# First blocks of one, two, three and four chunks on two queues, and the weight loads of the first stage moved behind them

## The chip, the cores and the metric

The kernel runs on one core of a Trainium2 chip. The metric is device time in microseconds (us), the median of several runs; lower is better. The engines are TensorE (PE: matmuls, with PEld for its weight loads), VectorE (DVE), ScalarE (ACT), GpSimd (POOL) and SyncE (SP). DMAs are issued from SP, from ACT and from POOL; in the profile SPq and ACTq are the issuing queues.

## The reference, cut to what matters

`x` is 2708 x 256 and `adj` a sparse 2708 x 2708 matrix, both float32. Four graph layers follow one another, each with a residual and a layernorm. Only the first and the start of the second matter here:

```python
# layer 0
x = _layernorm(x + adj @ (x * W0), axis=-1)
# layer 1 (graph attention, 4 heads of 64)
h = (x @ W).reshape(n, heads, head_dim)
src = einsum('nhd,d->nh', h, a[:head_dim, 0])
dst = einsum('nhd,d->nh', h, a[head_dim:, 0])
e = leaky_relu(src[:, :, None] + dst.T[None, :, :])     # masked by adj > 0, softmax, times h
x = _layernorm(x + _layernorm(out) * gamma + beta)
```

Layer 2 is three attention heads and two GRU cells, with weights `gat_W`, `gat_a` and biases `bih`, `bhh`; layer 3 is a mean over neighbours with two linear maps, `neigh_W` and `lin_W`.

## The kernel before, in words

Rows are cut into 22 tiles of 128 (the last has 20). The transposed adjacency comes in strips: strip t is 128 partitions x 22 chunks x 128 columns (1.44 MB), and layer 0 of row tile t is 22 matmuls of its chunks with the 22 chunks of x (`x0e`, kept in the tile `turn` with a column of ones for the degrees). A float32 matmul is two passes in the profile, so a strip is 44 passes.

Names and lines (those of the kernel before):

- L396 `w1_a` (ACT queue): W of layer 1, loaded first of all; L443 `w0_b`: W0 in all partitions; L498 `a1_b`: the attention vector; L215/L513 `wk`, `ak`: three heads' `gat_W` and `gat_a`; L233 `braw` in `gru_columns`: four bias vectors turned into columns, 3 KB each in pieces of 4 bytes. All these are issued from ACT before its first computation.
- L502/L509 fold `a1_b` into `w1_a` and L515/L516 make `uw` from `wk` and `ak`, on DVE; L234 to L239 make the bias columns `b_edge`, `b_node`.
- L524, L529 and L531, the prologue: for each block of four chunks SP loads the chunks of x and then the same chunks of strips 0, 1 and 2 (`ahead = 3`); L533 are their matmuls, L451 the mask (`adj > 0`) on DVE. Six blocks: five of four chunks, one of two.
- `layer0_own`: L458 takes the diagonal, L465 `below` makes six ACT passes over a strip that sum what is negative, 0.62 to 0.75 us each.
- L539: strip 3 whole, then L215 `nw` and `lw`, the weights of layer 3, from SP. L548: POOL writes `lwn_d` from `lw`.
- L202 `load_strip`: strips 4 to 21, in the two buffers that strips 0 and 1 leave; L211 their matmuls.
- `layer0_rest`: the layernorm (L170 to L175, its power `bn_rs` on POOL, L481) and then `layer1_projection`: PE transposes the tile (L187), ACT copies it to `xt` (L189), PE multiplies by `w1_a` (L419 `pm`), ACT makes `rise`, `h`, `fall` (L422 to L425), PE transposes `fall` (L434 `pf`).

Each engine runs its instructions in one order, which the scheduler fixes when the program is built; on ACT the first copy to `xt` stands behind the `below` passes of strips 0 to 4 and behind two of strip 5. The DMAs of SP and ACT take eight completion semaphores in turn, so each of them first waits until the DMA eight places before it, on whichever of the two queues, has landed. Instructions that the scheduler has moved apart from their place in the text are in the profile under the same lines.

Of the kernel before, what the change touches and what calls it, by code (L numbers as in the profile page):

```python
# [27 lines left out]
def kernel(  # L28
# [39 lines left out]

    sizes = [NT // -(-NT // GT) + (i < NT % -(-NT // GT)) for i in range(-(-NT // GT))]
    spans = [(sum(sizes[:i]), sum(sizes[: i + 1])) for i in range(len(sizes))]  # L70
    blocks = [(c, min(c + CB, NT)) for c in range(0, NT, CB)]


    NH, MH = N // 2, NT // 2
# [13 lines left out]
    def sz(i):  # L88
        return min(P, N - i * P)
# [4 lines left out]
    def bcast(row, n):  # L94
        return bass.AP(tensor=row.tensor, offset=row.offset, ap=[[0, P], [1, n]])
# [113 lines left out]
    def strip_matmul(acc, s, n, rhs):  # L209
        for c in range(NT):  # L210
            nc.tensor.matmul(acc, s[:, c, :n], rhs(c), start=(c == 0), stop=(c == NT - 1))  # L211

    def weights(pool, name, w, queue=nc.sync):
        wt = pool.tile([P, w.shape[0] // P, w.shape[1]], F32, name=name)
        queue.dma_start(wt, w.rearrange("(c p) j -> p c j", p=P))  # L215
        return wt
# [9 lines left out]
        nc.vector.tensor_tensor(y[:n], y[:n], pz[:n, :F], ALU.add)  # L226
        nc.scalar.dma_start(y3_d[t], y[:n])

    def gru_columns(pool, b, bih, bhh):

        raw = pool.tile([P, 2, 3 * FC], F32, tag="braw", name="braw", bufs=2)
        for i, src in enumerate((bih, bhh)):
            nc.scalar.dma_start(raw[:, i], src.rearrange("(c p) -> p c", p=P))  # L233
        nc.vector.tensor_tensor(raw[:, 0, : 2 * FC], raw[:, 0, : 2 * FC], raw[:, 1, : 2 * FC], ALU.add)  # L234
        nc.vector.tensor_scalar(
            b[:, 0:2].rearrange("p a c -> p (a c)"), raw[:, 0, : 2 * FC], 0.5, None, ALU.mult
        )
        nc.vector.tensor_scalar(b[:, 2], raw[:, 1, 2 * FC :], 0.5, None, ALU.mult)
        nc.vector.tensor_copy(b[:, 3], raw[:, 0, 2 * FC :])  # L239
# [153 lines left out]
    if True:  # L393

        w1_a = keep.tile([P, FC, F + 2 * H], F32, name="w1_a")
        nc.scalar.dma_start(w1_a[:, :, H : H + F], w1.rearrange("(c p) j -> p c j", p=P))  # L396

        hs = [keep.tile([P, H, HD + 1], F32, name=f"h{t}") for t in range(NT)]
        nc.gpsimd.memset(hs[NT - 1], 0.0)
# [7 lines left out]
        if True:  # L407
# [32 lines left out]
                    load_fall(falls[g // 2], g, nc.gpsimd)  # L440

            w0_b = keep.tile([P, F], F32, name="w0_b")
            nc.scalar.dma_start(w0_b, bcast(w0, F))  # L443
            quarter = keep.tile([P, CT], F32, name="quarter")
            nc.vector.tensor_reduce(quarter, ident.rearrange("p (j i) -> p i j", i=CT), AX.X, ALU.add)

            with pool("l0", 2) as l0:

                def layer0_mask(t, s, lo=0, hi=NT):
                    n = sz(t)  # L450
                    nc.vector.tensor_scalar(  # L451
                        mask[:, lo:hi, t * P : t * P + n], s[:, lo:hi, :n], 0.0, None, ALU.is_gt, saturate=False
                    )

                def layer0_own(t, s):
                    n = sz(t)
                    dtmp = st.rearrange("p t i k -> p (t i k)")
                    nc.vector.scalar_tensor_tensor(  # L458
                        dtmp[:n, :n], s[:n, t, :n], 1.0, ident[:n, :n], ALU.mult, ALU.mult,
                        accum_out=diag[:n, t : t + 1],  # L460
                    )
                    for i in range(BELOW):
                        lo, hi = i * NT // BELOW, (i + 1) * NT // BELOW
                        below = l0.tile([P, -(-NT // BELOW) * P], BF16, tag="below", name="below", bufs=1)
                        nc.scalar.activation(  # L465
                            below[:, : (hi - lo) * P], s[:, lo:hi].rearrange("p c n -> p (c n)"), AF.Relu, scale=-1.0,
                            accum_out=negative[:, BELOW * t + i : BELOW * t + i + 1],
                        )
# [25 lines left out]

                ahead = 3
                with pool("prep", side="right") as prep:
                    a1_b = prep.tile([P, 2 * HD], F32, name="a1_b")
                    nc.scalar.dma_start(a1_b, bcast(a1, 2 * HD))  # L498
                    for f in range(FC):
                        for s in range(2):  # L500
                            tmp = prep.tile([P, H, HD], F32, tag="t1", name="t1")
# [5 lines left out]
                            )  # L507
                            at = s * (H + F)
                            nc.vector.tensor_reduce(w1_a[:, f, at : at + H], tmp, AX.X, ALU.add)  # L509
                    for k in range(K):  # L510
                        wk = weights(prep, f"wk{k}", gat_w[k], nc.scalar)
                        ak = prep.tile([P, F], F32, name=f"ak{k}")
                        nc.scalar.dma_start(ak, bcast(gat_a[k], F))  # L513
                        tmp = prep.tile([P, FC, F], F32, tag="t2", name="t2")
                        nc.vector.tensor_tensor(tmp, wk, ak[:, None, :].to_broadcast([P, FC, F]), ALU.mult)  # L515
                        nc.vector.tensor_reduce(uw[:, :, k], tmp, AX.X, ALU.add)  # L516
                    gru_columns(prep, b_edge, e_bih, e_bhh)
                    gru_columns(prep, b_node, n_bih, n_bhh)
                    strips = [l0.tile([P, NT, P], F32, tag="strip", name="strip", bufs=2) for _ in range(2)]
                    strips += [prep.tile([P, NT, P], F32, name=f"strip{t}") for t in range(2, ahead + 1)]  # L520
                    accs = [ps_acc.tile([P, 512], F32, tag="acc", name="acc") for _ in range(ahead)]
                    for c0, c1 in blocks:
                        whole = min(c1, N // P)
                        nc.sync.dma_start(  # L524
                            turn[:, c0 * FE : whole * FE].rearrange("p (c f) -> p c f", f=FE)[:, :, :F],
                            x[c0 * P : whole * P, :].rearrange("(c p) f -> p c f", p=P),
                        )
                        for c in range(whole, c1):
                            nc.sync.dma_start(x0[c][: sz(c)], x[c * P : c * P + sz(c), :])  # L529
                        for t in range(ahead):  # L530
                            nc.sync.dma_start(strips[t][:, c0:c1], adj_t[t, :, c0:c1])  # L531
                            for c in range(c0, c1):
                                nc.tensor.matmul(  # L533
                                    accs[t][:, :FE], strips[t][:, c], x0e[c], start=(c == 0), stop=(c == NT - 1)
                                )
                            layer0_mask(t, strips[t], c0, c1)
                    for t in range(ahead):
                        layer0_own(t, strips[t])
                    nc.sync.dma_start(strips[ahead], adj_t[ahead])  # L539
                    for t in range(ahead):  # L540
                        layer0_scale(t, accs[t])
                    acc = ps_acc.tile([P, 512], F32, tag="acc", name="acc")
                    strip_matmul(acc[:, :FE], strips[ahead], P, lambda c: x0e[c])
                    for t in range(ahead):
                        finish(layer0_rest(l0, t))
                    nw = weights(prep, "nw", neigh_w)
                    lw = weights(prep, "lw", lin_w)
                    nc.gpsimd.dma_start(lwn_d[:, :, :F], lw[:, :FC])  # L548
# [1082 lines left out]
```

## Time and profile before

| what | value |
|---|---|
| median of 3 runs | 1880.27 us (1879.21 to 1880.66) |
| the profiled execution | 1881.39 us, of which the span is 1879.3 us |
| PE busy | 1840.5 us, 98% of the span |
| DVE, ACT, POOL busy | 1279.0, 689.0, 259.9 us |
| granted TensorE clock | 0.998 of full |
| DMA | 235.92 MB, mean 126 GB/s |
| PE busy in the first 15 us | 7.68 us |
| PE busy from 15 to 30 us, from 30 to 50 us | 13.94 of 15 us, 20.00 of 20 us |
| DMA in the first 30 us | 0.83 to 1.01 of the engines' time, 254 and 318 GB/s in the two halves |

Busy time is the union of an engine's instructions; matmuls overlap in their pipeline, so a matmul of 379 ns takes some 217 ns of PE's time in a row. An idle time of an engine is put down to what came last of what it waited for.

### The profile page before, as it was taken

What the parts mean: (1) busy time and instruction counts of PE and PEld (TensorE: products, weight loads), DVE (VectorE), ACT (ScalarE), POOL (GpSimd) and SP (SyncE); (2) the same over time, 40 slices, a digit from 0 to 9 for tenths busy, and PEclk for the clock granted to TensorE, in tenths of its full rate; (3) what the DMA queues carried; (4) which work ended last, traced back from release to release, by engine and by line L of the source; (5) the groups of instructions that cost most, each with busy time, mean ns of one, the idle gap of its engine ahead of it and who ended that gap; (6) DMA issues with size and microseconds to landing.
All of it is one profiled execution on the core that took longest, in us unless ns stands there. A gap on an engine that the chain in (4) does not pass through costs nothing.

```text
span 1879.3 us, 23102 instructions
## 1 busy us (share of the span) xinstructions
PE 1840.5 (98%) x7561; PEld 1035.5 (55%) x7565; DVE 1279.0 (68%) x2280; ACT 689.0 (37%) x1419; POOL 259.9 (14%) x419
## 2 busy tenths in 40 slices
PE   8999999999999999999999999999999999999997
PEld 7788842233345886887444444444445555554555
DVE  5343479999897655654658888776887758744664
ACT  4444410033144203111555665555564555311011
POOL 1211220001012411000011001210200202111111
PEclk9999999999999999999999999999999999999999
DMA  9344410100002657764557665454554445534764
GB/s 298 130 146 146 159 42 1 30 1 12 12 7 74 144 143 188 176 144 113 164 148 207 179 168 147 134 155 115 163 144 114 128 103 134 155 101 109 198 167 123
DMA packets 434204, 235.92 MB, mean 126 GB/s; under 512 B 184182, under 2 KB 421388, under 8 KB 431644
## 3 DMA queue, kind: packets, MB, share of 16 engines
q1 hardware_dynamic: 417438, 207.41, 40.5%
q0 software_dynamic: 7760, 21.20, 3.5%
q10 hardware_dynamic: 8878, 5.76, 1.0%
q8 instruction: 62, 1.02, 0.2%
q14 instruction: 66, 0.54, 0.1%
HBM read 221.61 MB, written 12.65 MB: 125 GB/s over the span
## 4 chain that ended last, share of the span: by engine, by line
PE 83%; DMA 5%; DVE 4%; issue 3%; ACT 2%; POOL 1%; SPq 1%; ACTq 0%; DVEq 0%; POOLq 0%
PE m L317 38%; PE acc L763 11%; PE bank L1128 7%; PE acc L211 7%; PE den L772 6%; PE gate L1003 4%; PE bank L1104 3%; DMA strip<-in_adj_t_dram 2%; PE bank L1179 1%; ACT below L465 1%; DMA p<-in_adj_t_dram 1%; SPq L264 1%; PE pm L419 1%; POOL bn_rs L175 1%; PE pq L929 1%
## 5 line engine op out<-in xcount | busy, mean ns | idle before, releaser
L781 DVE SCALAR_TENSOR_TENSOR p<-fall_b,rise,mask 128x1024 f32<-128x1024 f32 (+1 forms) x264 | 294.0, 1157 | 32.5 <-PE den L772 16.7
L1258 ACT ACTIVATE p<-st,e_neg 128x1024 f32<-128x1024 f32 (+1 forms) x198 | 197.1, 1040 | 193.7 <-PE m L317 186.3
L317 PE MATMUL m<-s,xq 128*128 128x512 f32 (+3 forms) x660 | 230.1, 467 | 0.0
L763 PE MATMUL acc<-p,h 128*64 128x512 f32 (+2 forms) x1056 | 214.5, 548 | 0.2 <-ACT sum L794 0.2
L317 PE MATMUL m<-p,xq 128*128 128x512 f32 (+1 forms) x396 | 182.8, 543 | 0.1
L211 PE MATMUL acc<-turn,strip 128*128 128x257 f32 x792 | 181.5, 379 | 0.0
L1261 ACT ACTIVATE p<-p 128x1024 f32<-128x1024 f32 (+1 forms) x198 | 178.9, 943 | 0.2
L1262 DVE TENSOR_TENSOR p<-p,blk 128x1024 f32<-128x1024 f32 (+1 forms) x132 | 143.6, 1107 | 39.7 <-ACT p L1261 24.3
L317 PE MATMUL m<-p,x 128*128 128x512 f32 (+1 forms) x396 | 167.8, 542 | 0.3 <-DVE supt L334 0.3
L304 DVE TENSOR_TENSOR s<-p 128x512 f32<-128x512 f32 (+3 forms) x132 | 81.1, 615 | 124.3 <-PE m L317 101.0
L317 PEld LDWEIGHTS m<-s,xq 128*128 128x128 f32 x660 | 124.3, 190 | 74.8 <-issue 57.6
L211 PEld LDWEIGHTS acc<-turn,strip 128*128 128x128 f32 x792 | 147.2, 190 | 20.3
L763 PEld LDWEIGHTS acc<-p,h 128*64 128x64 f32 x1056 | 69.8, 136 | 138.2 <-issue 128.6
L317 PE MATMUL m<-s,x 128*128 128x512 f32 (+3 forms) x330 | 127.3, 467 | 0.0
L772 PE MATMUL den<-p,h 128*32 128x512 f32 (+2 forms) x1056 | 117.7, 548 | 0.0
L317 PEld LDWEIGHTS m<-p,xq 128*128 128x128 f32 x396 | 74.6, 190 | 76.0 <-issue 61.4
L317 PEld LDWEIGHTS m<-p,x 128*128 128x128 f32 x396 | 74.4, 190 | 73.6 <-issue 61.2
L465 ACT ACTIVATE below<-strip 128x384 bf16<-128x384 f32 x132 | 78.5, 594 | 72.9 <-DMA strip<-in_adj_t_dram 69.5
L1262 DVE TENSOR_TENSOR p<-p,turn 128x1024 f32<-128x1024 f32 (+1 forms) x66 | 72.2, 1108 | 17.9 <-PE m L317 11.6
L305 DVE TENSOR_TENSOR p<-p 128x512 f32<-128x512 f32 (+3 forms) x132 | 82.4, 625 | 1.9
L307 DVE TENSOR_TENSOR s<-p,s 128x512 f32<-128x512 f32 (+3 forms) x132 | 81.5, 617 | 2.0
L317 PEld LDWEIGHTS m<-s,x 128*128 128x128 f32 x330 | 61.8, 190 | 38.1 <-issue 34.3
(276 smaller groups left out, 2541.1 us busy)
## 6 DMA issues: line engine op xcount, KB each, us to landing
strip<-in_adj_t_dram SPq DMA_DIRECT2D x19, 1408.0 KB, 6.0
blk<-in_adj_t_dram SPq DMA_DIRECT2D x88, 256.0 KB, 3.4
blk<-in_adj_t_dram SPq DMA_DIRECT2D x88, 192.0 KB, 4.0
pa<-in_adj_t_dram SPq DMA_DIRECT2D x110, 128.0 KB, 2.7
turn<-in_adj_t_dram SPq DMA_DIRECT2D x44, 256.0 KB, 3.3
blk<-in_adj_t_dram SPq DMA_DIRECT2D x88, 128.0 KB, 2.5
p<-in_adj_t_dram SPq DMA_DIRECT2D x88, 128.0 KB, 2.6
turn<-in_adj_t_dram SPq DMA_DIRECT2D x44, 192.0 KB, 3.1
```

What stands on the lines that cost most here:

```text
L211: nc.tensor.matmul(acc, s[:, c, :n], rhs(c), start=(c == 0), stop=(c == NT - 1))
L305: nc.vector.tensor_tensor(a21, a21, a11, ALU.subtract)
L307: nc.vector.tensor_tensor(s4, a12, s2, ALU.subtract)
L317: nc.tensor.matmul(dst[:, :w], lt, rt, start=start and not (one_bank and i), stop=stop and not (one_bank and i in (1, 2, 5)))
L465: nc.scalar.activation(below[:, : (hi - lo) * P], s[:, lo:hi].rearrange("p c n -> p (c n)"), AF.Relu, scale=-1.0, accum_out=negative[:, BE ...
L763: nc.tensor.matmul(acc[s][i * HD : (i + 1) * HD, :ws], hs[c][:, 2 * q + i, :HD], ps[i][:, p0 : p0 + ws], **flags,)
L772: nc.tensor.matmul(den[j : j + CT, :ws], hs[c][:, 2 * q + i, HD + 1 - CT :], ps[i][:, p0 : p0 + ws], **flags,)
L781: nc.vector.scalar_tensor_tensor(p[:, :w], falls[g // 2][:, 2 * q + i, :w], rise[:, c, 2 * q + i : 2 * q + i + 1], mask[:, c, at : at + w] ...
L1128: nc.tensor.matmul(g[:, :w], lt, rt, start=(q == 0), stop=(q == len(terms) - 1))
L1258: nc.scalar.activation(p[:, :, :w], st_k[:, :, :w], AF.Relu, scale=-1.0, bias=e_neg[:, at, k : k + 1])
L1261: nc.scalar.activation(p[:, :, :w], p[:, :, :w], AF.Exp, scale=-1.0)
L1262: nc.vector.tensor_tensor(p[:, :, :w], p[:, :, :w], blk[:, i, :, :w], ALU.mult)
```

## The change

The blocks become 1, 2, 3, 4, 4, 4, 4 chunks. The x chunks of the first two blocks are issued from ACT, all the rest from SP. The block loop is moved ahead of the weight preparation, and `w0_b`, then strip 3, then `w1_a`, `a1_b`, `wk`, `ak` and the biases are issued from SP behind the last block (`tc.issue_after` only fixes that order in the queue); `gru_columns` is cut in two, the loads (`gru_load`) and the arithmetic. The DVE arithmetic on the weights moves behind strip 3's mask. `nw`, `lw` and the strips from 4 on follow in SP's queue as before. In the new order of ACT, the first copy to `xt` stands behind the passes of strips 0 to 4 and four of strip 5; PE, POOL and the later parts of all engines keep their order but for one chunk of strip 4, which PE takes later.

```diff
--- before.py
+++ after.py
@@ -68,7 +68,8 @@
 
     sizes = [NT // -(-NT // GT) + (i < NT % -(-NT // GT)) for i in range(-(-NT // GT))]
     spans = [(sum(sizes[:i]), sum(sizes[: i + 1])) for i in range(len(sizes))]
-    blocks = [(c, min(c + CB, NT)) for c in range(0, NT, CB)]
+    cuts = [0, 1, 3, 6, *range(10, NT, CB), NT]
+    blocks = list(zip(cuts, cuts[1:]))
 
 
     NH, MH = N // 2, NT // 2
@@ -226,11 +227,15 @@
         nc.vector.tensor_tensor(y[:n], y[:n], pz[:n, :F], ALU.add)
         nc.scalar.dma_start(y3_d[t], y[:n])
 
-    def gru_columns(pool, b, bih, bhh):
+    def gru_load(pool, bih, bhh):
 
         raw = pool.tile([P, 2, 3 * FC], F32, tag="braw", name="braw", bufs=2)
         for i, src in enumerate((bih, bhh)):
-            nc.scalar.dma_start(raw[:, i], src.rearrange("(c p) -> p c", p=P))
+            nc.sync.dma_start(raw[:, i], src.rearrange("(c p) -> p c", p=P))
+        return raw
+
+    def gru_columns(b, raw):
+
         nc.vector.tensor_tensor(raw[:, 0, : 2 * FC], raw[:, 0, : 2 * FC], raw[:, 1, : 2 * FC], ALU.add)
         nc.vector.tensor_scalar(
             b[:, 0:2].rearrange("p a c -> p (a c)"), raw[:, 0, : 2 * FC], 0.5, None, ALU.mult
@@ -393,7 +398,6 @@
     if True:
 
         w1_a = keep.tile([P, FC, F + 2 * H], F32, name="w1_a")
-        nc.scalar.dma_start(w1_a[:, :, H : H + F], w1.rearrange("(c p) j -> p c j", p=P))
 
         hs = [keep.tile([P, H, HD + 1], F32, name=f"h{t}") for t in range(NT)]
         nc.gpsimd.memset(hs[NT - 1], 0.0)
@@ -440,7 +444,6 @@
                     load_fall(falls[g // 2], g, nc.gpsimd)
 
             w0_b = keep.tile([P, F], F32, name="w0_b")
-            nc.scalar.dma_start(w0_b, bcast(w0, F))
             quarter = keep.tile([P, CT], F32, name="quarter")
             nc.vector.tensor_reduce(quarter, ident.rearrange("p (j i) -> p i j", i=CT), AX.X, ALU.add)
 
@@ -494,8 +497,45 @@
 
                 ahead = 3
                 with pool("prep", side="right") as prep:
-                    a1_b = prep.tile([P, 2 * HD], F32, name="a1_b")
-                    nc.scalar.dma_start(a1_b, bcast(a1, 2 * HD))
+                    strips = [l0.tile([P, NT, P], F32, tag="strip", name="strip", bufs=2) for _ in range(2)]
+                    strips += [prep.tile([P, NT, P], F32, name=f"strip{t}") for t in range(2, ahead + 1)]
+                    accs = [ps_acc.tile([P, 512], F32, tag="acc", name="acc") for _ in range(ahead)]
+                    for c0, c1 in blocks:
+                        whole = min(c1, N // P)
+                        queue = nc.scalar if c1 <= 3 else nc.sync
+                        queue.dma_start(
+                            turn[:, c0 * FE : whole * FE].rearrange("p (c f) -> p c f", f=FE)[:, :, :F],
+                            x[c0 * P : whole * P, :].rearrange("(c p) f -> p c f", p=P),
+                        )
+                        for c in range(whole, c1):
+                            nc.sync.dma_start(x0[c][: sz(c)], x[c * P : c * P + sz(c), :])
+                        for t in range(ahead):
+                            landed = nc.sync.dma_start(strips[t][:, c0:c1], adj_t[t, :, c0:c1])
+                            for c in range(c0, c1):
+                                nc.tensor.matmul(
+                                    accs[t][:, :FE], strips[t][:, c], x0e[c], start=(c == 0), stop=(c == NT - 1)
+                                )
+                            layer0_mask(t, strips[t], c0, c1)
+                    for t in range(ahead):
+                        layer0_own(t, strips[t])
+                    with tc.issue_after(landed.ins):
+                        nc.sync.dma_start(w0_b, bcast(w0, F))
+                        landed = nc.sync.dma_start(strips[ahead], adj_t[ahead])
+                    with tc.issue_after(landed.ins):
+                        nc.sync.dma_start(w1_a[:, :, H : H + F], w1.rearrange("(c p) j -> p c j", p=P))
+                        a1_b = prep.tile([P, 2 * HD], F32, name="a1_b")
+                        nc.sync.dma_start(a1_b, bcast(a1, 2 * HD))
+                        gats = []
+                        for k in range(K):
+                            wk = weights(prep, f"wk{k}", gat_w[k])
+                            ak = prep.tile([P, F], F32, name=f"ak{k}")
+                            nc.sync.dma_start(ak, bcast(gat_a[k], F))
+                            gats.append((wk, ak))
+                        bias = [gru_load(prep, *ab) for ab in ((e_bih, e_bhh), (n_bih, n_bhh))]
+                    for t in range(ahead):
+                        layer0_scale(t, accs[t])
+                    acc = ps_acc.tile([P, 512], F32, tag="acc", name="acc")
+                    strip_matmul(acc[:, :FE], strips[ahead], P, lambda c: x0e[c])
                     for f in range(FC):
                         for s in range(2):
                             tmp = prep.tile([P, H, HD], F32, tag="t1", name="t1")
@@ -507,42 +547,14 @@
                             )
                             at = s * (H + F)
                             nc.vector.tensor_reduce(w1_a[:, f, at : at + H], tmp, AX.X, ALU.add)
-                    for k in range(K):
-                        wk = weights(prep, f"wk{k}", gat_w[k], nc.scalar)
-                        ak = prep.tile([P, F], F32, name=f"ak{k}")
-                        nc.scalar.dma_start(ak, bcast(gat_a[k], F))
+                    for t in range(ahead):
+                        finish(layer0_rest(l0, t))
+                    for k, (wk, ak) in enumerate(gats):
                         tmp = prep.tile([P, FC, F], F32, tag="t2", name="t2")
                         nc.vector.tensor_tensor(tmp, wk, ak[:, None, :].to_broadcast([P, FC, F]), ALU.mult)
                         nc.vector.tensor_reduce(uw[:, :, k], tmp, AX.X, ALU.add)
-                    gru_columns(prep, b_edge, e_bih, e_bhh)
-                    gru_columns(prep, b_node, n_bih, n_bhh)
-                    strips = [l0.tile([P, NT, P], F32, tag="strip", name="strip", bufs=2) for _ in range(2)]
-                    strips += [prep.tile([P, NT, P], F32, name=f"strip{t}") for t in range(2, ahead + 1)]
-                    accs = [ps_acc.tile([P, 512], F32, tag="acc", name="acc") for _ in range(ahead)]
-                    for c0, c1 in blocks:
-                        whole = min(c1, N // P)
-                        nc.sync.dma_start(
-                            turn[:, c0 * FE : whole * FE].rearrange("p (c f) -> p c f", f=FE)[:, :, :F],
-                            x[c0 * P : whole * P, :].rearrange("(c p) f -> p c f", p=P),
-                        )
-                        for c in range(whole, c1):
-                            nc.sync.dma_start(x0[c][: sz(c)], x[c * P : c * P + sz(c), :])
-                        for t in range(ahead):
-                            nc.sync.dma_start(strips[t][:, c0:c1], adj_t[t, :, c0:c1])
-                            for c in range(c0, c1):
-                                nc.tensor.matmul(
-                                    accs[t][:, :FE], strips[t][:, c], x0e[c], start=(c == 0), stop=(c == NT - 1)
-                                )
-                            layer0_mask(t, strips[t], c0, c1)
-                    for t in range(ahead):
-                        layer0_own(t, strips[t])
-                    nc.sync.dma_start(strips[ahead], adj_t[ahead])
-                    for t in range(ahead):
-                        layer0_scale(t, accs[t])
-                    acc = ps_acc.tile([P, 512], F32, tag="acc", name="acc")
-                    strip_matmul(acc[:, :FE], strips[ahead], P, lambda c: x0e[c])
-                    for t in range(ahead):
-                        finish(layer0_rest(l0, t))
+                    for b, raw in zip((b_edge, b_node), bias):
+                        gru_columns(b, raw)
                     nw = weights(prep, "nw", neigh_w)
                     lw = weights(prep, "lw", lin_w)
                     nc.gpsimd.dma_start(lwn_d[:, :, :F], lw[:, :FC])
```

## The prediction

> **What bounds the kernel now.** I read the slices first: TensorE (PE) is busy in every slice but the first, so the 1879.3 us span moves only if PE's idle time moves. Then PE's waits over the first 110 us (what waited for what: us in total, times, longest), and its timeline (start, length, group, count, idle time before it):
>
> ```profile
> PE acc L533 <- DMA strip<-in_adj_t_dram: 8.4, 2, 6.6
> PE pm L419 <- ACT xt L189: 1.0, 1, 1.0
> ```
>
> ```profile
> 6.62 7.68 PE L533 MATMUL acc<-turn,strip 128*128 128x257 f32 x24 [6.62 <-DMA strip<-in_adj_t_dram]
> 16.06 23.71 PE L533 MATMUL acc<-turn,strip 128*128 128x257 f32 x108 [1.76 <-DMA strip<-in_adj_t_dram]
> 39.61 9.73 PE L211 MATMUL acc<-turn,strip 128*128 128x257 f32 x44
> ...
> 51.44 1.16 PE L419 MATMUL pm<-w_a,xt 128*128 128x264 f32 x4 [1.01 <-ACT xt L189]
> ```
>
> There are two losses to the strip transfers (6.62 and 1.76 us), and then a wait at 51.44 for another reason: ScalarE (ACT) had not copied the first `xt`. The second block came late for a reason in SyncE's (SP) own waits, where x stood behind a weight of the ACT queue:
>
> ```profile
> SPq L524 <- DMA a_b<-in_L_gnn_a_dram: 3.2, 1, 3.2
> ```
>
> Why the copy was late is in the chain, which runs over DMAs to lw, then over ACT's `below` passes without a break, to the copy:
>
> ```profile
> 31.05 6.91 DMA lw<-in_L_gnn_lin_W_dram
> ...
> 49.76 0.62 ACT below L465 x2
> 50.40 0.72 ACT below L465 x2
> 51.13 0.26 ACT xt L189
> ```
>
> ACT started strip 0's last piece at 31.75 and never caught up; the copy ended at 51.39. From 60 to 80 us PE is busy 20.00 of 20 us and from 100 to 150 us 49.50 of 50, so what the first projection gains, the end gains.
>
> The rates come from the windows view (columns: stretch, length, busy and count of PE, PEld, DVE, ACT, POOL, clock, DMA share, GB/s):
>
> ```profile
> 6.00:9.00 3.00, 2.38 (x6) 1.95 (x7) 0.00 (x0) 0.00 (x0) 0.00 (x0) 1.00 0.72 189
> 13.50:18.00 4.50, 2.74 (x13) 2.12 (x12) 3.13 (x11) 2.46 (x5) 0.00 (x0) 1.00 1.06 198
> 18.00:30.00 12.00, 12.00 (x57) 10.45 (x56) 5.80 (x24) 1.81 (x7) 0.00 (x0) 1.00 1.02 356
> 9.00:12.00 3.00, 3.00 (x11) 2.42 (x10) 2.90 (x7) 0.00 (x0) 0.00 (x0) 1.00 1.08 379
> 33.00:36.00 3.00, 3.00 (x16) 2.61 (x15) 0.05 (x1) 2.87 (x10) 0.00 (x0) 1.00 0.95 387
> ```
>
> So 356 GB/s for blocks alone, 379 with 1 KB weight rows, 387 for a whole strip.
>
> [...] some ten matmul passes at 635 ns, then 379 ns. [...] Here strip 3 (issued 29.62) landed at 35.95, lw (31.05) at 37.96. [...] the 3 KB `braw` loads, in 4-byte pieces, took 5.4 to 6.0 us to land.
>
> **The change, part by part.**
>
> (1) The start. 131 KB of x and 66 KB of a strip come first, on two queues. Nearest row: gamma_b (131 KB, quiet queue) landed 2.9 us after issue; issued at 0.74, x is there at about 3.6 (bounds 3.2 and 5). The 132 passes cost 10 x 0.43 cold and 122 x 0.217 (23.71/108 less the tail), 30.7 us. They are fed: four chunks take PE 5.2 us, and 1.31 MB at 356 GB/s takes 3.7. SP waits for the transfer eight before (eight semaphores in turn), never longer than that. Blocks end at 34.3 (before: 39.4), strip 3's 9.7 us at 44.0, two transposes and four passes (1.1) at 45.1, against 50.4. **Alone this is worth 5.3 us, 6.3 with the 1.0 us wait gone.**
>
> (2) The moved loads. On SP all now lie ahead of strips 4 and 5. The blocks are 2.77 + 4.33 = 7.1 MB: 0.14 MB by 3.0 us, the rest at 356 GB/s, 22.5; 0.1 for the smaller pieces, 22.6 (before, the last mask of the blocks began near 32.4). w0_b and strip 3, 1.57 MB at 387: 26.7. w1_a, wk, ak, 1.44 MB at 379: 30.5. a1_b is 66 KB, 0.2 us by bytes; but in 6 to 9 us, its time in flight, DMA moved 0.57 MB, worth 1.6 us of 3, so up to 1.6 us: I take 0.8, 31.3. The four `braw` loads: 13.5 to 18 us moved 0.89 MB, 2.5 us' worth, so 2.0 us net, 4.5 if nothing overlaps them in one queue; I take 3.0, 34.3. nw and lw, 0.79 MB: **36.4, within 34.8 and 38.7**. Before it was 37.96: the weights that left the front came back ahead of strip 4.
>
> (3) Strips 4 and 5 wait for PE's last pass on strips 0 and 1 (about 30.8 and 32.5) and are then in SP's queue, so they follow lw. The pair before: issued 38.11, landed 48.19, less 1.2 us before data flows, so 4.4 us each, lwn_d's write inside. Strip 4 lands at 40.8, strip 5 at 45.2. ACT's order is fixed: six `below` pieces of strip 4 (4.32), four of strip 5 (2.74), then `xt` (0.26): lw's end + 11.7 = **48.1, within 46.5 and 50.4**. PE is there at 45.1 and waits about 3 us. So of 6.3 us, 51.4 - 48.1 = 3.3 stay.
>
> (4) Hidden work. ACT's 13 issues become two; its first `below` waits for strips anyway, and it is done with strip 3 at 35.7, idle until strip 4. VectorE's 8 + 6 + 8 preparation steps (3.4 + 4.1 + 1.3 us) now precede the layernorms and end with the last `braw`, 34.8 at the latest here; POOL's `bn_rs` stands behind lwn_d's issue, so behind lw (36.4 + 0.4). The first x is normalised near 38.5, needed at 44.0. Without that slack each microsecond would go to PE's transposes, still under ACT's lateness. SP's 13 more weight issues (0.33 to 0.5 us) lie under its 6.0 us wait for PE at L202. Between `xt` and `fall`, ACT has two `below` pieces instead of three and PE one chunk less, which shows up later: 0.08 us, nothing. The rest of the order is unchanged on all engines.
>
> Sum: the profiled execution took 1881.39 us (span 1879.3 and 2.1 around it), 1.1 above the median of 1880.27; less 3.3 it gives 1878.1. On the median: **1877.0 us**. A measurement of this kernel can tell about 0.2%, 3.8 us, from no change; the gain falls just short of that.
>
> **The rivals.** *A, the queue clears early*: bytes alone count for a1_b and `braw`, lw is in at 34.8, `xt` at 46.5: 4.9 us, 1875.4. For it: DMA share was 1.06 in the `braw` stretch, so other bytes shared that time; against it: it moved only 198 GB/s[...]. *B, `braw` blocks SP (slower)*: one such issue took long:
>
> ```profile
> 13.10 2.37 ACTq L233 DMA_DIRECT2D braw<-in_L_gnn_node_bhh_dram  x1
> ```
>
> If all four take 2.37 us, starting when w1_a has landed (27.9), nw is issued at 37.4, lw ends at 41.0, `xt` at 52.7: 1.3 us slower, 1881.6. It turns to a loss when nw is issued later than 36.1, and passes 0.2% if each issue takes 3.0 us or more. Against it: the other three took 0.37 to 0.44. *C, the start does not move*[...]: PE comes up to 3 us later, at 48, still no later than `xt`: 1877 again. *D, ACT is not held* (strips 4 and 5 land by 37): 6.3 us, 1874.0; the queue order speaks against it.
>
> **How the numbers follow.** The forecast 0.50, A 0.24, D 0.05, C 0.11, B 0.10. Part of the forecast's own range (46.5 to 50.4) lies beyond 3.8 us. Faster by over 0.2%: A, D and 0.04 of the forecast, 0.33; slower by over 0.2%: the worse part of B and the unforeseen, 0.08; within: 0.59. The range 1874.8 to 1881.6 reaches from just short of D to B's price.
>
> **What would show it.** Right: the first matmul near 3.6, PE's 1.76 us wait gone, blocks done near 34, and a wait of PE pm for ACT `xt` of about 3 us, with ACT waiting for strip 4 after strip 3; lw landing at 35 to 39. Wrong: no such wait (D), or SP issues of `braw` of 2 us (B), or waits after 60 us that were not there before.

## The result, and the profile after

The changed kernel takes 1883.5 us in the median (1881.0 to 1885.4, 22 runs) against 1879.5 for the kernel before on the same chip: a ratio of 1.0018 [1.0012, 1.0024], slower by 0.18%. The forecast was 1877.0, so it is 6.5 us off. The profiled execution took 1882.37 us, with a span of 1880.2.

The start went as planned. PE's waits over the first 110 us (what waited for what: us in total, times, longest) and its timeline (start, length, group, count, idle time before):

```profile
PE pm L423 <- ACT xt L190: 4.9, 1, 4.9
PE acc L515 <- DMA turn<-in_x_dram: 3.5, 1, 3.5
```

```profile
3.46 30.73 PE L515 MATMUL acc<-turn,strip 128*128 128x257 f32 x132 [3.46 <-DMA turn<-in_x_dram]
34.03 9.72 PE L212 MATMUL acc<-turn,strip 128*128 128x257 f32 x44
...
49.72 2.12 PE L423 MATMUL pm<-w_a,xt 128*128 128x264 f32 x4 [4.87 <-ACT xt L190]
```

PE starts at 3.46 us instead of 6.62, never waits in the blocks, and is done with them at 34.0 instead of 39.6. Then it stands still for 4.87 us at the first projection, and the four passes of `pm` take 2.12 us instead of 1.16: they run at half clock. ACT's timeline shows why the copy is late, the `below` passes of strip 4 starting when it lands, then those of strip 5, then the copy:

```profile
42.20 0.52 ACT L468 ACTIVATE below<-strip 128x384 bf16<-128x384 f32 x1 [5.41 <-DMA strip<-in_adj_t_dram]
...
46.64 0.52 ACT L468 ACTIVATE below<-strip 128x384 bf16<-128x384 f32 x1 [0.15 <-DMA strip<-in_adj_t_dram]
...
49.31 0.35 ACT L190 COPY xt<-tr 128x256 f32<-128x256 f32 x1
```

The clock is in the windows view (stretch, length, busy and count of PE, PEld, DVE, ACT, POOL, clock, DMA share, GB/s):

```profile
44.00:47.00 3.00, 0.84 (x4) 0.39 (x3) 1.98 (x4) 2.75 (x9) 0.00 (x0) 1.00 0.62 239
47.00:50.00 3.00, 0.28 (x1) 0.28 (x2) 2.86 (x9) 2.90 (x10) 0.00 (x0) 0.65 0.00 0
50.00:53.00 3.00, 3.00 (x9) 2.15 (x10) 0.98 (x3) 1.36 (x8) 0.55 (x1) 0.50 0.00 0
53.00:56.00 3.00, 3.00 (x12) 2.43 (x10) 0.00 (x0) 0.70 (x4) 0.57 (x1) 0.71 0.01 1
```

The granted clock fell to half during the wait, at 47.9, and came back at 54.7, so the work that had waited ran slowly. A landmark tells the balance: PE begins to transpose its seventh row tile, here called x_83, at 99.61 us before and at 99.60 after. **The whole early gain is gone by 100 us**, and more is lost later: 0.9 us between this pair of profiles, 4.0 by the medians. One profile is one draw: a second profile of the kernel before (e5) took 1879.52 us where the first took 1881.39, and its x_83 is at 99.62 too; against that one 2.7 us are lost later.

### The profile page after: what moved, and what is told of

It reads as the page before. It is cut to its first block, busy times and chain, and to the rows that moved or that the text cites. A ratio compares the mean times of both kernels' runs of the same rounds, so it can differ in the third digit from the quotient of the medians.

```text
span 1880.2 us, 23115 instructions
## 1 busy us (share of the span) xinstructions
PE 1840.5 (98%) x7565; PEld 1037.6 (55%) x7565; DVE 1281.9 (68%) x2283; ACT 690.0 (37%) x1419; POOL 254.3 (14%) x419
## 4 chain that ended last, share of the span: by engine, by line
PE 84%; DMA 5%; DVE 4%; issue 3%; ACT 2%; POOL 1%; SPq 1%; POOLq 0%; DVEq 0%; ACTq 0%
PE m L322 38%; PE acc L775 11%; PE acc L212 8%; PE bank L1140 7%; PE den L784 6%; PE gate L1015 4%; PE bank L1116 3%; DMA strip<-in_adj_t_dram 3%; PE bank L1191 1%; SPq L269 1%; PE pm L423 1%; DMA p<-in_adj_t_dram 1%; POOL bn_rs L176 1%; PE pq L941 1%; DVE p L1274 1%
## 5 line engine op out<-in xcount | busy, mean ns | idle before, releaser
L322 PEld LDWEIGHTS m<-s,x 128*128 128x128 f32 x330 | 61.8, 190 | 38.1 <-issue 34.3
```

The source lines that it names most:

```text
L322: nc.tensor.matmul(dst[:, :w], lt, rt, start=start and not (one_bank and i), stop=stop and not (one_bank and i in (1, 2, 5)))
```

## The experiments

"x_83" is that landmark, and "pm" the start of the first projection. All ratios are to the kernel before on the same chip, with their 95% interval.

### e1 to e4: is it the wait, the clock or the bias loads?

**e1** is the changed kernel once more.

> The changed kernel once more, with a second profile. Clock theory: PE again waits 4 to 5.5 us at the first pm, and the granted clock falls to one half near the end of that wait and comes back 3.4 or 6.8 us later[...]. Rival (loss elsewhere): the part beyond the first 67 us is longer than in the kernel before by 2 to 3 us. Both: 1.001 to 1.003 of the kernel before.

1.0014 [1.0008, 1.0021]; PE waited 4.56 us, pm at 50.29, the clock was at half for 3.41 us, x_83 at 99.23. The wait repeats. So does the loss that the rival named: the part behind x_83 is 1.6 us longer than in the first profile of the kernel before, 3.5 longer than in e5.

**e2** gives PE filler during the wait:

```diff
+                if t == 0:
+                    for _ in range(9):
+                        nc.tensor.matmul(pm[:, :FE], ident, x0e[0], start=True, stop=True)
                 for f in range(FC):
```

> The changed kernel with nine added matmuls (18 passes, 3.9 us, results overwritten) between the first transposes and the first pm, so that PE waits about 2 us instead of 4.9 for the copy to xt. Clock theory: the copy still ends near 49.7, but the clock stays full, and the passes after it run at 0.22 us instead of 0.43; two chunks (0.9 us) move behind the wait. The stage ends 1.5 to 2.5 us earlier than in the changed kernel: 0.999 to 1.0005 of the kernel before. Rival (only the wait itself counts, or the loss is elsewhere): no gain against the changed kernel, or 0.9 us slower.

1.0018 [1.0010, 1.0026]; x_83 at 99.44, no gain, so the expectation was missed. The filler ended at 47.5, PE still waited 1.97 us, and the clock fell all the same, at 50.8, after pm had run. The timeline and the windows show it:

```profile
49.45 1.16 PE L426 MATMUL pm<-w_a,xt 128*128 128x264 f32 x4 [1.97 <-ACT xt L190]
```

```profile
50.00:53.00 3.00, 3.00 (x12) 2.28 (x11) 0.84 (x2) 1.55 (x8) 0.77 (x2) 0.63 0.00 0
```

Where the clock falls has an order in the traces. In the changed kernel it first rises at 6.93, falls at 47.89, 12 steps of 3.41 us later, rises again at 54.72, two steps on, and falls at the end, at 1870.61, after 546 steps; in the kernel before 545 steps lie between its rise at 11.15 and its fall at 1871.42. PE's work in single steps of that length, for e2 (first fence) and for e15 (second; its edit is told below), where PE waited longer, 2.30 us, and the clock held:

```profile
47.37:50.78 3.41, 1.44 (x7) 1.06 (x6) 2.48 (x10) 3.32 (x13) 0.55 (x1) 1.00 0.00 0
50.78:54.19 3.41, 3.41 (x11) 2.62 (x10) 0.43 (x1) 0.81 (x5) 0.57 (x1) 0.50 0.02 5
```

```profile
49.76:53.17 3.41, 2.56 (x13) 1.88 (x11) 2.55 (x9) 3.25 (x11) 0.01 (x1) 1.00 0.13 32
53.17:56.58 3.41, 1.96 (x10) 1.47 (x11) 0.84 (x2) 2.39 (x11) 0.54 (x1) 1.00 0.18 44
```

The 1.97 us of e2 lie in one step; the 2.30 us of e15 are split, 0.85 and 1.45. Waits of 1.97 us (e2), 2.62 (e3), 3.72 (e11), 4.56 (e1), 4.87 (the changed kernel) and 5.21 (e14) were followed by half clock; those of 1.86 us (e7) and 2.30 (e15) were not.

**e3** leaves the four bias loads out (the biases are taken as zero):

```diff
-            nc.sync.dma_start(raw[:, i], src.rearrange("(c p) -> p c", p=P))
+            nc.gpsimd.memset(raw[:, i], 0.0)
```

> The changed kernel without the four bias loads (4-byte pieces); zeros stand in their place, so the biases are left out. Queue theory: nw, lw and strips 4 and 5 land 3 to 4 us earlier, the copy to xt ends near 46, PE waits about 1.3 us and keeps its clock: 5 to 7 us faster than the changed kernel, 0.997 to 0.999 of the kernel before. Rival (the bias loads cost only their 0.01 MB): under 1 us. Rival (loss elsewhere, not before 67 us): the stage gains, the end stays above the kernel before.

1.0000 [0.9992, 1.0009]; pm at 47.82 after a wait of 2.62 us, x_83 at 96.94, less than expected. Strip 4 comes 2.5 us earlier than in the changed kernel:

```profile
39.67 0.52 ACT L468 ACTIVATE below<-strip 128x384 bf16<-128x384 f32 x1 [3.02 <-DMA strip<-in_adj_t_dram]
...
47.42 0.35 ACT L190 COPY xt<-tr 128x256 f32<-128x256 f32 x1
```

So the bias loads hold up the queue by about 2.5 us. The copy gains only 1.9 of it, because in this kernel's order of ACT it stands behind five pieces of strip 5 and not four. The clock still fell.

**e4** puts strip 4's load and its 22 matmuls ahead of the first projections:

```diff
                     strip_matmul(acc[:, :FE], strips[ahead], P, lambda c: x0e[c])
+                    s4 = load_strip(l0, ahead + 1)
+                    last, acc = acc, ps_acc.tile([P, 512], F32, tag="acc", name="acc")
+                    strip_matmul(acc[:, :FE], s4, P, lambda c: x0e[c])
...
-                for t in range(ahead + 1, NT - 1):
+                layer0_scale(ahead, last)
+                finish(layer0_rest(l0, ahead))
+                for t in range(ahead + 2, NT - 1):
```

> The changed kernel with all 22 chunks of strip 4 ahead of the first three projections in PE's order; all loads stay as they are in the queue. If the loss is PE's wait for the copy to xt and the clock that it costs, PE now has 9.6 us of work over the time in which the copy was late: no wait at pm, no fall of the clock, strip 4's landing (42.2) is just before PE needs it (43.6). Then 6 to 7.5 us are gained against the changed kernel's profile, and it is 0.996 to 0.998 of the kernel before (1873 to 1876). Rival (the late strips only move the wait to strip 5 or 6): a wait of 2 us or more at acc L212, and less than 3 us of gain.

0.9981 [0.9972, 0.9989], just outside the 0.996 to 0.998 expected, x_83 at 93.20. The loads are as late as in the changed kernel, but PE has work to cover them, and the clock holds:

```profile
35.26 19.29 PE L212 MATMUL acc<-turn,strip 128*128 128x257 f32 x88
54.38 0.38 PE L188 MATMUL tr<-ident,x 128*128 128x128 f32 x2
```

So the change and this edit together are worth 6.4 us at x_83 (e7 divides the two); of these the ratio keeps 3.6 at the end.

### e5 to e8: which half of the change, and the clock

**e5**, the kernel before once more.

> The kernel before, unchanged, for a second profile. The profiled execution of the kernel before that we compare with was 1.1 to 1.8 us above its median, while that of the changed kernel was 1.1 us below its own; stage by stage the changed kernel stood at 0.0 us against it at 100 us, -1.2 us from 700 to 1440 us, and lost 0.9 us at 1491 us and 0.8 us at 1720 us. Theory 'scatter': the early stretch repeats within 0.5 us (first matmul 6.6, first projection 51.4, transpose of x_83 at 99.6), and the differences after 100 us are another draw of the same waits, so this profile differs from the first one by 1 to 2 us in the same places. Rival 'the change costs something late': this profile repeats the first one within 0.5 us at every stage, the +0.9 at 1491 and +0.8 at 1720 then belong to the change. Ratio 1.000 in either case.

1.0000 [0.9992, 1.0008]. The early stretch repeats, and from 660 us on this profile stands 1.3 us ahead of the first one, 1.9 at the end. Against it the changed kernel loses 2.7 us after x_83, most of which the first profile of before had hidden: some 0.6 near 1490 us, 0.8 near 1721 us (e13) and 1.1 at the very end (e10).

**e6**, the changed kernel with the old blocks of four:

```diff
-    cuts = [0, 1, 3, 6, *range(10, NT, CB), NT]
-    blocks = list(zip(cuts, cuts[1:]))
+    blocks = [(c, min(c + CB, NT)) for c in range(0, NT, CB)]
```

> The changed kernel with the old blocks of 4 chunks, all of x over SP's queue: the weights stay queued behind the strips. Theory (the first projection is set by the transfers of the queue and by ACT's below passes, not by the start): the first matmul comes about 5 us, the blocks end near 36, strip 3 near 45.5, but lw lands and xt is copied when they were in the changed kernel, 49 to 50; PE waits about 3 us instead of 4.9, the clock still falls for 3.4 us or more, x_83 is transposed at 99.2 to 99.6: ratio as for the changed kernel, 1.0010 to 1.0025. So the small first blocks are worth nothing. Rival (the small blocks do count): everything comes 1.5 to 2 us later than in the changed kernel, x_83 near 101, ratio 1.0025 to 1.0035.

1.0001 [0.9993, 1.0010]. Both theories missed: x_83 is at 95.64, 4 us ahead of the changed kernel. (This profile is a draw on the fast side: 1878.57 us, where the 13 runs have a median of 1880.37 and reach 1883.41.) The first matmul comes at 5.45, the blocks end 2.6 us later, yet ACT's copy comes 1.86 us earlier:

```profile
41.86 0.52 ACT L467 ACTIVATE below<-strip 128x384 bf16<-128x384 f32 x1 [6.34 <-DMA strip<-in_adj_t_dram]
...
47.45 0.35 ACT L189 COPY xt<-tr 128x256 f32<-128x256 f32 x1
```

Of that, 0.34 us is strip 4 (41.86 against 42.20). The rest is ACT's order: here the copy stands behind two pieces of strip 5, in the changed kernel behind four. PE waits only 0.43 us, and the clock holds. The windows view of the changed kernel (first fence) and of e6 (second) shows slower transfers with the small pieces:

```profile
3.00:6.00 3.00, 2.54 (x6) 2.11 (x7) 2.02 (x4) 0.36 (x1) 1.66 (x3) 1.00 0.96 283
6.00:9.00 3.00, 3.00 (x13) 2.45 (x12) 0.59 (x2) 1.53 (x3) 0.00 (x0) 1.00 0.90 267
```

```profile
3.00:6.00 3.00, 0.55 (x1) 0.50 (x2) 0.43 (x1) 0.61 (x1) 1.65 (x3) 1.00 1.07 391
6.00:9.00 3.00, 3.00 (x8) 2.35 (x7) 1.60 (x7) 1.36 (x4) 0.00 (x0) 1.00 1.07 373
```

That is 275 GB/s on average instead of 382. A strip piece of one chunk is 512 bytes in a row, one of four chunks 2 KB; the runs do not separate the length of the rows from the number of loads. The 4 us don't last: against e5 the lead of e6's profile is 4.0 us at x_83, about 2 us from 840 us on, and 0.8 us at the end.

**e7**, e4's edit on the kernel before.

> The kernel before with the load and the 22 matmuls of strip 4 ahead of the first projections, as in e4; loads and blocks otherwise as before. In e4 the same edit on the changed kernel gave -6.4 us at x_83 and a ratio of 0.9981. Theory (the edit by itself is worth only the wait that it covers): here the covered wait is 1.0 us plus 0.2, so -1.2 us at x_83 and a ratio of 0.9993; the other 5 us of e4 are then the change's early start, kept once PE has something to do. Rival (the edit by itself brings more, for example because ACT's below passes no longer stand ahead of the copies): -4 us or more, ratio 0.998.

0.9994 [0.9985, 1.0002], x_83 at 97.00 (-2.6). The ratio is the theory's; the landmark moved twice as far as it said. The larger part of e4's gain at x_83, 3.8 of 6.4 us, comes with the change (its early start and its moved loads together).

**e8**, e2 with `range(16)`.

> The changed kernel with 16 instead of 9 passes of filler before the first pm (they write the pm bank, which is started anew afterwards). With 9, PE still waited 1.97 us and the clock fell to half for 3.4 us. The filler now ends near 49.1, so PE's wait is under 0.6 us. Theory (a wait of about 2 us is what brings the clock down, and the drop costs 1.5 to 2.5 us): no half clock near 50, the first pm still starts at 49.1 to 49.6, x_83 at 97.0 to 98.0 instead of 99.2 to 99.6, ratio 1.0002 to 1.0010. Rival (the loss lies in the late ACT chain and not in the clock): x_83 stays at 99.2 or later, ratio 1.0015 or more.

1.0015 [1.0009, 1.0022], x_83 at 100.12. These are the rival's numbers, for another reason. The filler was mis-sized: each of its matmuls is two passes, so it ran to 51.8 and delayed pm itself, to 51.80. The clock held. From pm to x_83 took 48.3 us.

### e9 to e12: the stop at the end, ACT's order, a better version

**e9**, e2 with `range(12)`.

> The changed kernel with 12 passes-pairs of filler before the first pm (each float32 matmul is two passes, 0.44 us together; with 16 the filler ran on to 51.8 and so started the first pm 2 us late itself, with 9 it left a wait of 1.97 us and the clock fell). It should end near 48.9 to 50.2, PE then waits under 0.6 us. Theory (the clock's fall costs 1 to 2 us, since from the first pm to the transpose of x_83 the clock-held e8 took 48.3 us and the changed kernel 49.9): no half clock near 50, x_83 at 97.5 to 98.5 instead of 99.2 to 99.6, ratio 1.0005 to 1.0011. Rival (no cost of the clock): x_83 at 99.2 or later, ratio 1.0014 or more.

1.0009 [1.0001, 1.0017]; pm at 49.89 after 0.2 us of waiting, clock held, x_83 at 98.83, 0.3 us later than expected. What a fall costs is read from pm to x_83, between kernels that do the same work there without other waits. With 172 passes over strips, e15, whose clock held, took 47.6 us; e1, e3 and e11, with half clock for 3.41 us, took 48.9 to 49.1; the changed kernel and e14, with 6.83 us of it, took 49.9 and 50.1. With 176 passes, e8 took 48.3 (held) and e2 50.0 (3.41 us). **In these runs a fall that lasted 3.41 us cost about 1.5 us, and one that lasted 6.83 about 2.4.** The kernel before, e5, e6, e9 and e10 held their clock too, but have small waits in this stretch and took 47.8 to 48.9, so less of the cost shows against them. By the ratio alone nothing is shown: e9's interval overlaps those of e1 and e2.

**e10**, the kernel before with 15 more DMA instructions on SP:

```diff
-                nc.sync.dma_start(gamma_b, bcast(gamma, F))
-                nc.sync.dma_start(beta_b, bcast(beta, F))
+                cut = [*range(0, F, 32), F - 16, F]
+                for a, z in zip(cut[:-2], [*cut[1:-2], F]):
+                    nc.sync.dma_start(gamma_b[:, a:z], bcast(gamma[a:z], z - a))
+                for a, z in zip(cut, cut[1:]):
+                    nc.sync.dma_start(beta_b[:, a:z], bcast(beta[a:z], z - a))
```

> The kernel before with gamma and beta loaded in 17 pieces instead of 2: 15 more DMA instructions on SP (1803 to 1818, as many as the changed kernel has), issued near 50 us where SP has nothing else to do; no other engine's order is touched. In every kernel with more than 1809 SP instructions (the changed one, e1 to e4, e6, e8) SP's closing row of semaphore waits stands still for 1.0 to 1.2 us before its 1810th instruction, and the end comes 6.5 to 6.7 us after the last store's issue; in before, e5 and e7 (1801 to 1803) it comes 5.4 to 5.5 us after. Theory (SP's longer program has one more stop, and at the end nothing hides it): here too 6.5 to 6.7 us, with the stop at the same place, ratio 1.0005 to 1.0008. Rival (the stop comes from what was moved, not from the number of instructions): 5.4 to 5.5 us, ratio 1.0000. If the later DMA order depends on the count as well, the layernorm at 1720 us also waits 0.5 to 0.8 us longer for its copy y.

The theory holds: the ratio, 1.0008 [1.0000, 1.0016], only just tells, but the end of the trace does. SP's last issue and the span, for e5, for the changed kernel and for e10:

```profile
core 0 of [0], span 1877.5 us
...
1872.07 0.33 SPq L1293 DMA_DIRECT2D out_dram<-y  x1
```

```profile
core 0 of [0], span 1880.2 us
...
1873.57 0.33 SPq L1305 DMA_DIRECT2D out_dram<-y  x1
```

```profile
core 0 of [0], span 1880.9 us
...
1874.27 0.33 SPq L1296 DMA_DIRECT2D out_dram<-y  x1
```

From the last issue to the end: 5.4, 6.6 and 6.6 us. SP closes with a row of semaphore waits, 0.06 to 0.1 us apart, and in the changed kernel two neighbours of the row start at 1877.89 and 1879.03. The second is the 1810th of SP's 1818 instructions. The extra instructions did not bring the wait near 1721 us that e14 and e13 speak of.

**e11**, the changed kernel with `queue = nc.sync` for all of x.

> The changed kernel with the first two x pieces issued from SP as the others are (small blocks and moved weights kept). The scheduler then puts ACT's first copy to xt behind two of strip 5's below pieces, as in the kernel before and in e6, and not behind four as in the changed kernel. Theory (those two pieces, 1.4 us, the wait of 4 to 5 us that they lengthen and the clock's fall are what separates e6 from the changed kernel): first matmul at 3.6 to 4.8, xt copied near 47.7, PE waits 2 to 3.5 us, the clock may fall for 3.4 us; x_83 at 96.0 to 98.2, ratio 1.0000 to 1.0006. Rival (the small pieces themselves slow the transfers, so that strip 4 and xt come late whatever ACT's order): xt at 49 or later, x_83 at 99 or later, ratio 1.0012 or more.

1.0004 [0.9995, 1.0012], x_83 at 98.50. Half of the theory fell: the copy does stand behind two pieces of strip 5, but strip 4 landed at 43.41, 1.5 us later than in e6, so `xt` was ready at 49.3 and PE waited 3.7 us. The strips do come late whatever ACT's order, as the rival said, though x_83 and the ratio stay short of its numbers; ACT's order is a second term.

**e12**, e4 with nine SP instructions fewer (1808):

```diff
-    cuts = [0, 1, 3, 6, *range(10, NT, CB), NT]
+    cuts = [0, 1, 3, 6, 10, 16, NT]
...
-                        nc.sync.dma_start(w0_b, bcast(w0, F))
+                        nc.scalar.dma_start(w0_b, bcast(w0, F))
...
+                        wks = prep.tile([P, K * FC, F], F32, name="wks")
+                        nc.sync.dma_start(wks, gat_w.rearrange("k (c p) j -> p (k c) j", p=P))
+                        aks = prep.tile([P, K, F], F32, name="aks")
+                        nc.sync.dma_start(aks, bcast_rows(gat_a, 0, F))
...
```

> e4 (strip 4 ahead of the first projections) with fewer SP instructions: the three wk and the three ak loaded by one DMA each, the last blocks cut at 6, 10, 16, 22 instead of every four chunks, w0_b from ACT's queue: nine fewer, 1808. Theory (count of SP instructions): the closing stop is gone, the end comes 5.4 to 5.5 us after the last store's issue instead of 6.56, the first 100 us as in e4 (x_83 at 93 to 94), ratio 0.9974, 1.1 us under e4. Rival (blocks of six chunks come late or the merged weights do): PE waits over 1 us in the prologue or at the first projection, ratio 0.9981 or more.

0.9963 [0.9950, 0.9977] where 0.9974 was expected, x_83 at 94.42, a little late; no stop, 5.6 us from the last issue to the end, and PE loses 1.0 us to a strip at the start, which the rival had feared:

```profile
6.47 30.16 PE L515 MATMUL acc<-turn,strip 128*128 128x257 f32 x128 [0.98 <-DMA strip<-in_adj_t_dram]
36.47 19.29 PE L212 MATMUL acc<-turn,strip 128*128 128x257 f32 x88
```

### e13 to e16: what was still open

**e13**, e12 with `queue = nc.sync` for all of x, and `a1_b` from ACT.

> e12 with all of x issued from SP, and a1_b from ACT instead (1809 SP instructions, so still no closing stop). In the eight kernels whose first x pieces come over ACT's queue (the changed one, e1 to e4, e8, e9, e12) PE waited 0.5 to 0.8 us longer near 1721 us for a layernorm behind the copy y; in the five others besides the second profile of the kernel before (before, e6, e7, e10, e11) it did not. Theory (it goes with that queue): no extra wait here at 1721, the end 0.5 to 0.8 us under e12 from there on, ratio 0.9960 to 0.9975. Rival (chance, or the number of DMAs): 0.5 us or more again. Either way the first 100 us should be as in e12, x_83 at 93.5 to 95.

0.9979 [0.9969, 0.9988], x_83 at 94.88. The extra wait near 1721 is gone, as the theory said, but the time is no better: this profile, 2.2 us above its own median, fell 1.8 us behind e12's near 730 us instead. What it was about, in e5 and in e1 (DVE's timeline):

```profile
1720.40 0.47 DVE L1160 SCALAR_TENSOR_TENSOR y<-bank,diag,x 20x256 f32<-20x256 f32 x1 [2.24 <-DMA y<-y]
```

```profile
1722.09 0.47 DVE L1172 SCALAR_TENSOR_TENSOR y<-bank,diag,x 20x256 f32<-20x256 f32 x1 [2.97 <-DMA y<-y]
```

The eight kernels with x on ACT's queue that the expectation names have it, 0.5 to 0.8 us later than in e5, and e16 has it too; the five others that it names have not, nor have e5 and e13. In these profiles the two go together; the mechanism is not shown.

**e14**, the changed kernel with e12's three edits and without strip 4 first.

> The changed kernel with e12's fewer SP instructions (1809 by count) but without strip 4 ahead of the projections. Theory (the stop comes before the 1810th SP instruction and costs 1.1 us): no stop here, the end 5.4 to 5.6 us after the last store's issue instead of 6.6. The scheduler puts the first xt behind five below pieces of strip 5 (four in the changed kernel), so PE waits 4.5 to 6 us, the clock falls and x_83 comes at 99.4 to 100.5: ratio 1.0008 to 1.0014. Rival (it is bytes or blocks that matter, not the count): the end again 6.6 us after the last store.

1.0003 [0.9994, 1.0011]. The stop is gone (5.4 us from the last issue to the end), though the copy comes later still (PE waits 5.2 us) and x_83 is at 101.62, 1.1 us beyond what was expected. The end did better than that landmark, by more than the stop; this profile, 1883.0 us, was 1.9 above its own median.

**e15**, the kernel before with the new cuts alone, all x from SP.

> The kernel before with the blocks of 1, 2, 3, 4 ... chunks, all x from SP, the weights still first on ACT's queue. Theory (PE starts earlier but the first xt is set by lw, strip 4 and ACT's pieces): first matmul at 3.5 to 5, blocks done at 37 to 39, the first xt behind five below pieces of strip 5 instead of two, so at 52 to 54; PE waits 3 to 6 us, the clock falls, x_83 at 101 to 103, ratio 1.0008 to 1.0020. Rival (an earlier start is an earlier end): x_83 at 98 or earlier, ratio 0.9995 or less.

1.0018 [1.0011, 1.0025], x_83 at 102.18; the rival fell. The blocks ended at 41.5, later than before (39.6) and not earlier as expected: PE lost 7.5 us to strips in five waits. ACT's copy at 54.22 cost another 2.3 us, and there the clock held, against what was expected.

**e16**, e12 once more.

> e12 once more, to have its ratio from more runs and its profile twice: both theories of the count and of strip 4 first expect 0.9963 to 0.9980, x_83 near 94.4, the end 5.4 to 5.6 us after the last store's issue, and again 0.5 us or more at 1721.

0.9968 [0.9956, 0.9980], x_83 at 95.53 (1.1 late), 5.4 us at the end, and 0.7 us at 1721. **The version to keep is e12**, some 0.3% faster than the kernel before.

## Why the prediction was wrong

**The step that failed** is "so what the first projection gains, the end gains". PE did begin the first projection earlier, at 49.72 us instead of 51.44, but by x_83 nothing was left of it, and behind x_83 time was lost. Two costs stood at nothing in the prediction's sum: what PE's wait does to its clock, and what more instructions do to SP. A third term, the time of the loads, was too small.

*Step 1, the start: right.* First matmul 3.46 (3.6), blocks done 34.03 (34.3), strip 3 43.6 (44.0), PE there at 44.85 (45.1). (The clock first rose 4.5 us after the first matmul before and 3.5 after; the sum took ten slow passes, 4.3 us, in both.) The wait on ACT came, so D fell; lw landed at 38.35 and not at 34.8, so A fell; and the bias issues took 1.1 us at most in the changed kernel, so B fell as well.

*Steps 2 and 3, the queue: right in kind, 1.6 us short.* Strip 4 landed at 42.20, not 40.8, and `xt` was done at 49.66, not 48.1, though inside the range to 50.4. The bias loads are not to blame: in e3, without them, lw lands 3.5 us earlier, of which the weights ahead of them account for 0.6, so they cost 2.9 us there against the 3.0 taken. The term that was mis-sized is the blocks: their last piece landed at 24.35 where the sum has 22.6. The prediction let them run at 356 GB/s from 3 us on; by 9 us the windows show (85 + 283 + 267) x 3 us, 1.9 MB, where its rate would have given 2.3, 1 us late. But by 21 us the bytes have caught up to within 0.5 us, so the first rate is only part of it. The sum counts bytes and the profile landings; what else held the landings back stays open. lw was then 1.95 us late; strip 4, which followed lw sooner than taken, 1.4.

*Missing: what the wait does to the clock.* The prediction took a wait of 3 us as 3 us: it counted slow passes at the start and none after the wait that it forecast. A wait of 1.97 us in e2 was followed by half clock, one of 1.86 in e7 was not. In the changed kernel 4.87 us of waiting brought 6.83 us of half clock, which cost 2.3 us against e15's stretch from pm to x_83, and 1.7 against that of the kernel before, which has small waits there.

*Missing: what more instructions cost.* Thirteen loads moved to SP, and two more issues, took its program from 1803 to 1818 instructions and brought a stop of 1.1 us in the closing waits, where nothing covers it: the end comes 6.6 us after the last issue in the changed kernel and in e10, which has as many instructions, and 5.4 in e14, which has 1809. "SP's 13 more weight issues (0.33 to 0.5 us) lie under its 6.0 us wait" priced each issue where it stands and not the length of the program. A further 0.8 us near 1721 us came with x on ACT's queue: the waits after 60 us that the prediction named as a sign of being wrong.

*The sum.* A gain of 3.3 us was forecast, and the medians on one chip show a loss of 4.0: 7.3 us have to be explained. (Against 1877.0 it is 6.5, because the median of the kernel before over 22 runs lies 0.7 us below that of the three runs that the forecast started from.) Up to x_83 the account closes: 1.6 us from the late `xt` and 1.7 from the clock. Behind it, 1.1 us are the stop and 0.8 the wait near 1721 us. That is 5.2 us; the remaining 2.1 us are not settled. Some 0.6 of them lie near 1490 us against e5, where waits differ between profiles without a cause that the runs show.

*The rivals.* C said that a start which does not move would give 1877 again. It did move, so C fell; but e6, whose start is 2 us later with the same moved loads, is faster than the changed kernel. That `xt` and not the start decides the first projection was right, and it reaches further than it was taken: the small blocks alone made the kernel slower (e15, in which ACT's order changed with them), and the moved weights alone, with the stop at the end among their costs, left it as it was (e6).

## What to carry to other kernels

An early start is worth what the next wait on that engine leaves of it: look for work that can stand between the two (strip 4 here) before moving loads. Count a forecast wait of the matmul engine as the wait and what the clock does afterwards (here 4.87 us of waiting brought 6.83 us of half clock). A gain at one landmark is not yet a gain at the end: follow it through later landmarks. When instructions are moved to a queue, count them too, and look at the last microseconds of the span (1803 instructions on SP became 1818 here, and 5.5 us from the last issue to the end became 6.6).

## What the runs showed of the hardware that was not expected

- In the changed kernel SP stopped for 1.14 us, from 1877.89 to 1879.03, ahead of the 1810th of its 1818 instructions. The expectation of e10 names six more kernels with a stop of 1.0 to 1.2 us at that place, and e10, with 1818 instructions, ended 6.6 us after its last issue, as the changed kernel did. The kernel before, with 1803, ended after 5.5 us (5.4 in e5), and e14, with 1809, after 5.4. The cause is not shown.
- The granted clock changed at steps of 3.41 us from its first rise in the changed kernel (after 12, 14 and 546 steps) and in the kernel before (after 545). A wait of 1.97 us (e2) brought it down, one of 1.86 us (e7) and one of 2.30 us (e15), split over two steps, did not. It came back after 3.41 us in e1 and e2, and after 6.83 us in the changed kernel.
- The scheduler's fixed order moved with each edit of the loads: the first copy to `xt` stands behind two (before, e6, e11), four (the changed kernel) or five pieces of strip 5 (e3, e14, e15), 0.65 to 0.75 us each. This is of the program and not of the chip, and it hides in a comparison.
